# Recording the first and second group norms in three steps instead of two, with the scale pinned on VectorE

## Chip, core and metric

The kernel runs on one core of a Trainium2 chip. Time is device microseconds of one launch, the median of several runs; the profile is one execution, with the span from its first to its last instruction. The core has five engines with a queue each: TensorE (PE: matmuls, with weight loads shown as PEld), VectorE (DVE), ScalarE (ACT), GpSimd (POOL) and SyncE (SP), which here only issues DMAs.

## What is computed

Two bottleneck blocks on an input of 64 images, 1024 channels, 14 x 14 positions. The first has batch norms over the whole batch; the second is deformable and has group norms, one set of statistics for each image and group:

```python
# first block
out = relu(_bn(_conv(x, w1, b1, 1, 0), g1, be1))
out = relu(_bn(_conv(out, w2, b2, 1, 1), g2, be2))
out = softplus(residual_scale)[0] * _bn(_conv(out, w3, b3, 1, 0), g3, be3)
x = relu(x + out)
# second block
out = relu(group_norm(conv(x, w1), gn1_scale, gn1_bias))
om = conv(out, w_off, pad=1) + b_off
sampled = bilinear_sample(out, py(om), px(om)) * sigmoid(om[:, 18:])
out = einsum('bckhw,ock->bohw', sampled, w2)
out = relu(group_norm(out, gn2_scale, gn2_bias))
out = group_norm(conv(out, w3), gn3_scale, gn3_bias)
return relu(out + x)
```

with

```python
def group_norm(x, scale, bias, groups=32, eps=1e-05):
    xg = x.reshape(B, groups, C // groups, H, W)
    m = xg.mean(axis=(2, 3, 4), keepdims=True)
    v = xg.var(axis=(2, 3, 4), keepdims=True)
    xn = ((xg - m) * rsqrt(v + eps)).reshape(B, C, H, W)
    return xn * scale + bias
```

## The kernel before

**Stages.** The first block takes roughly the first 970 us. The change is in the second, which goes through the batch in 32 pairs of images (`NP` = 32, `p` is the number of a pair; a tile row holds 2 x 196 positions). It is a software pipeline written out by hand: `slot(t)` does the sampling and the second convolution of pair t, and beside them the first convolution, the first norm and the offset convolution of pair t+1, and the second norm, the third convolution and the third norm of pair t-1. `fill()` stands ahead of the first slot, `tail()` behind the last. In slots 0 and 1 there is no first convolution (`d1` is empty), since `fill()` has done it.

**Order.** Each stage is a list of small functions ("steps"). `put(steps, extra, at)` places each of `extra` ahead of the step whose number is in `at`, and `weave` mixes two lists evenly; the calls of all of them in turn are the recorded order. Inside the slots only TensorE follows that order as recorded (`manual_schedule` names PE alone); for VectorE, ScalarE, GpSimd and SyncE a scheduler orders the instructions by its own estimate of when their inputs are there, earlier recorded ones first. `tc.keep_in_program_order(ins)` ties one instruction: it stays behind the instruction that was recorded last on its engine. In `tail()` PE, VectorE, GpSimd and ScalarE all follow the recorded order.

**The norm.** `Norm` keeps the statistics of one pair. `stats` (L1004) are `bn_stats` on VectorE, one for each image and block of 128 channels. `total` (L1015) is a transpose. `mean` is five VectorE instructions (L1025 to L1036). `root` is one on VectorE (L1041, maximum and epsilon) and a power on GpSimd (L1042). `scale` is a transpose (L1048) and three small instructions (L1057, L1060, L1063) on VectorE, which leave factor `sc` and shift `sh` for the activations on ScalarE. `scale` has a parameter `tie` for the transpose. `finish` is `root` and `scale`, one right behind the other. The third norm has its own steps (`total`, `mean`, `root`, `end`), with the scale tied; the first and second have `mean` and `finish`.

**What lies around it in a slot from t = 2 to t = 30**, in recorded order. First `d1`, 16 steps of two matmuls each (L1099): block 0 (steps 0 to 7), then block 1 (8 to 15); at the end of a block ScalarE copies the result (L1107) and VectorE takes its statistics. Into this list go the second norm's steps, at 6 the late output of pair t-2 (two sums on VectorE, L1745, each with an activation on ScalarE, L1747, and then the store, L1773, issued by SyncE), and at 10 the products for the first set of taps (`corners`, L1392, tied). The four activations of the second norm are L1576; from them GpSimd makes the sums T (L1592 to L1596).

Then come the sampling matmuls (`sp`, L1412, copied out by ScalarE, L1420) woven with the first half of the third convolution (`d`, L1655), 24 steps, and into them goes the first norm of pair t+1. The third convolution has seven products for each j, m = 0 to 6, in three banks of PSUM. Products 0 and 1 give E (copied by ScalarE, L1659). Products 2 and 3 give V on VectorE (L1662: bank plus E). After product 4 GpSimd makes two sums from V (L1667: a new E, and part of z). After product 5 VectorE writes z (L1671). Product 6 adds into the bank that V is read from, and L1675 writes the rest of z. In this list the products of j = 0 are steps 0, 2, 4, 6, 7, 9 and 11, those of j = 1 begin at step 12. The first norm's activations (L1122) go to steps 14, 16, 18 and 21; they feed the transforms (L1163, L1167) for the offset convolution (`om`, L1187).

The tiles z are two buffers, one for each half of the channels, which change owner every slot: the new z can be written when the old one's output has been stored.

Of the kernel before, what the change touches and what calls it, by code (L numbers as in the profile page):

```python
# [22 lines left out]
MB = 2  # L23
# [21 lines left out]
def kernel(  # L45
# [197 lines left out]
    with ExitStack() as l, tc.manual_schedule(  # L243
# [127 lines left out]
        for n in range(K):  # L371
            q, j = divmod(n, HB)
# [88 lines left out]
    with upool, tc.manual_schedule(  # L461
# [11 lines left out]
        sp = pool(upool, "s", 4)  # L473
# [181 lines left out]
    with l0, tc.manual_schedule(  # L655
# [107 lines left out]
        for p in range(2, NP - 2, 2):  # L763
            tt = Ts
            for j in range(HB):
                acc = [ps.tile([P, N2], FP, tag=f"ps{m}", name=f"c3_{p}_{j}_{m}") for m in range(4)]
                part = ts(j, P)
# [157 lines left out]
    def build_second_bottleneck(l1, path, run, early):  # L925
# [56 lines left out]
        class Norm:  # L982
# [79 lines left out]
                )  # L1062
                nc.vector.tensor_tensor(self.sh, self.sh, beta, ALU.add)  # L1063

            def finish(self):
                self.root()
                self.scale()

        pairs = {}
# [10 lines left out]
        def residual(p, b0=0, b1=CB):  # L1082

            for b in range(b0, b1):

                tc.keep_in_program_order(end_of_first(p, Z0, b))
                relu_of_first(p, b)

        def first_conv(p, by_inputs=False):
# [22 lines left out]
                order.sort(key=lambda v: v[1])  # L1112
            return [lambda o=o, c=c: step(o, c) for o, c in order]

        def first_norm(p):
            q = pairs[p]

            def relu(c, i):
                n, a1 = q["gn1"], q["a1"]

                tc.keep_in_program_order(
                    nc.scalar.activation(  # L1122
                        a1[:, c, ts(i, HW)],
                        a1[:, c, ts(i, HW)],
                        AF.Relu,
                        bias=n.sh[:, c, i : i + 1],
                        scale=n.sc[:, c, i : i + 1],
                    )
                )
                if i == 1:  # L1130
                    transform(p, c)

            return [lambda: q["gn1"].mean(), lambda: q["gn1"].finish()] + [
                lambda c=c, i=i: relu(c, i) for c in range(MB) for i in range(2)
            ]

# [432 lines left out]
        def second_norm(p, m=0):  # L1569

            q = pairs[p]

            def relu(c, i):
                n, h2 = q["gn2"][m], q["h2"]
                b = c - n.b0
                nc.scalar.activation(  # L1576
                    h2[:, c, ts(i, HW)],
                    h2[:, c, ts(i, HW)],
                    AF.Relu,
                    bias=n.sh[:, b, i : i + 1],  # L1580
                    scale=n.sc[:, b, i : i + 1],
                )

            def sums():
                if p == NP - 1:
                    return
                h2 = q["h2"]
                T3 = q["T3"] = {
                    m: one.tile([P, HW], FP, tag=f"T{m}", name=f"T{m}_{p}") for m in (1, 2, 4)
                }  # L1590
                (b11, b12), (b21, b22) = ([h2[:, c, ts(i, HW)] for i in range(2)] for c in range(2))
                nc.gpsimd.tensor_tensor(T3[1], b12, b11, ALU.subtract)  # L1592
                nc.gpsimd.tensor_tensor(T3[2], b22, T3[1], ALU.subtract)

                nc.gpsimd.tensor_tensor(b12, b22, b12, ALU.subtract)
                nc.gpsimd.tensor_tensor(T3[4], b21, T3[2], ALU.subtract)  # L1596

            order = ((0, 0), (0, 1), (1, 1), (1, 0))
            if p == NP - 1:
                order = ((m, 0), (m, 1))  # L1600
            return (
                [lambda: q["gn2"][m].mean(), lambda: q["gn2"][m].finish()]
                + [lambda c=c, i=i: relu(c, i) for c, i in order]
                + [sums]
            )
# [175 lines left out]
        def weave(a, b):  # L1781

            both = [((n + 0.5) / len(l), m, s) for m, l in enumerate((a, b)) for n, s in enumerate(l)]
            return [s for _, _, s in sorted(both, key=lambda v: v[:2])]

        def put(steps, extra, at):

            done, at = [], at[: len(extra)]
            for n, s in enumerate(steps):
                done += [extra[m] for m, k in enumerate(at) if k == n]  # L1790
                done.append(s)
            return done + [extra[m] for m, k in enumerate(at) if k >= len(steps)]
# [11 lines left out]
        def slot(t):  # L1804
# [5 lines left out]
            def part(yes, stage, *args):  # L1810
                return stage(*args) if yes else []
# [7 lines left out]
            for e in range(2, E):  # L1819
                sp[e - 2].append(lambda e=e: this and (list(spread_rows(t, e)), list(spread_columns(t, e)), corners(t, e)))  # L1820
            d1 = part(front and not (early and t < 2), first_conv, t + 1)
            norm1, norm2, norm3 = (
                part(front, first_norm, t + 1)[2 if early and t == 1 else 0 :],
                part(back, second_norm, t - 1),
                part(back, third_norm, t - 1),
            )
# [9 lines left out]
            om = part(front, offset_conv, t + 1) + part(front, selection, t + 1) + loads  # L1836
            half = len(d3) // 2
            if d1:
                extra = list(zip((5, 8, 12, 12, 13, 13, 14), norm2)) + [(10, w) for w in weights[:1]]
                extra = sorted(extra + [(6, s) for s in late], key=lambda v: v[0])  # L1840
                todo = put(d1, [s for _, s in extra], [k for k, _ in extra])
                todo += put(weave(sp[0], d3[:half]), norm1, (4, 7, 14, 16, 18, 21))
                todo += weights[1:] + d3[half : half + 2] + om
                todo += weave(sp[1], d3[half + 2 :])
            else:
                extra = list(zip((3, 6, 8, 9, 10, 10, 10), norm2)) + list(zip((0, 0, 1, 1), norm1))
                extra = sorted(
                    extra + [(9, w) for w in weights[1:]] + [(4, s) for s in late], key=lambda v: v[0]
                )
                todo = put(sp[0], [s for _, s in extra], [k for k, _ in extra])  # L1850
                todo += om + weave(sp[1], d3[:half]) + d3[half:]
# [28 lines left out]
            extra = []  # L1880
            if early and t == 0:

                extra += list(zip((5, 11), first_norm(2)))
            if bare:
                extra.append((n - 6, lambda: corners(t + 1, 0)))
            if back and t < NP - 1:
# [2 lines left out]
                extra.append((3, lambda: output(t - 1, 1)))  # L1889
            if t == NP - 1:  # L1890

                extra += list(zip([n // 2 + k for k in (3, 5, 6, 6)], ends2))
            extra.sort(key=lambda v: v[0])
            todo += put(pd[E - 1], [s for _, s in extra], [k for k, _ in extra])
            if ahead:
# [4 lines left out]
        def tail():  # L1900

            p = NP - 1
            mean, finish2, *relus = second_norm(p, 1)[:-1]
            d3 = plain_third_conv(p)

            def products(first, end):
                for step in d3[first:end]:
                    step()

            def ends(n, b0, b1):  # L1910
                for b in range(b0, b1):
                    finish(p, n, b)

            products(0, 3)
            mean()
            products(3, 5)
            finish2()
            for step in relus:
                step()
            products(5, 10)  # L1920
            n0, n1, n2 = pairs[p]["gn3"]
            n0.total()
            products(10, 12)
            n0.mean()
            products(12, 14)
            n0.root()
            n1.total()
            products(14, 15)
            n1.mean()
            n0.scale()  # L1930
            products(15, 16)
            n1.root()
            n2.total()
            n2.mean()
            ends(n0, 0, 1)
            n2.root()
            n1.scale()
            ends(n0, 1, 4)
            store(p, 0, 4)
            n2.scale()  # L1940
            ends(n1, 0, 2)
            store(p, 4, 6)
            ends(n2, 0, 2)
            store(p, 6, 8)
# [11 lines left out]
        def fill():  # L1956

            for p in range(3):
                start(p)
            load_h3(2, Z0)  # L1960
            steps = first_conv(0, by_inputs=True)
            norm = first_norm(0)
            steps += put(
                first_conv(1),
                norm[:2] + [offset_weights] + norm[2:] + offset_conv(0) + selection(0),
                (3, 5, 5, 6, 6, 6, 6) + (12,) * (MB * 3) + (12,),
            )
            norm, (distances, end) = first_norm(1), factors(0)
            steps += [lambda: pairs[1]["gn1"].total(), lambda: residual(2, 0, 3)] + transposes(0)

            steps += norm[:1] + [lambda: residual(2, 3, 7), distances, lambda: residual(2, 7), end]

            def spread():

                for e in range(2):
                    for n, _ in enumerate(zip(spread_rows(0, e), spread_columns(0, e))):
                        if e == n == 0:
                            lend(0)

            steps += [spread]  # L1980
            steps += put(
                first_conv(2),
                norm[1:]
                + [lambda: sums_of_second(0, 3), lambda: corners(0, 0)]
                + offset_conv(1)
                + selection(1)
                + [lambda: sums_of_second(6)],
                (3, 7, 7, 8, 8, 11, 11) + (12,) * (MB * 3) + (14, 16),
            )
            for step in steps:  # L1990
                step()
# [94 lines left out]
```

## Time and profile before

| | |
|---|---|
| median of 3 runs | 2870.07 us (2866.82 to 2872.13) |
| profiled execution | 2869.56 us, its span 2867.8 us |
| mean granted TensorE clock | 0.992 |
| busy, share of the span: PE / PEld | 97% / 70% |
| VectorE / ScalarE / GpSimd | 82% / 46% / 32% |
| DMA, mean rate over the span | 148 GB/s |

A timeline row gives start, length, engine, line and operation, then what is written from what, with partitions and elements, and how many instructions the row merges; in brackets stands the idle time of the engine ahead of it and what ended that. Instructions of one engine can overlap by a little, and TensorE's ends are modelled, so durations on TensorE are best taken from start to start.

### The profile page before, as it was taken

The numbers are of one execution on the slowest core, as the hardware profiler recorded it, in microseconds if no ns is written. First come the engines' busy times: TensorE is split into PE (matmuls) and PEld (weight loads), VectorE is DVE, ScalarE is ACT, GpSimd is POOL, SyncE is SP. The second block draws the span as 40 slices with busy tenths as digits, with TensorE's granted clock in tenths as the row PEclk, the third lists the DMA queues.
The fourth block names the chain that finished last, engine by engine and source line by source line (L and its number), as shares of the span: only waits on it lengthen the run. The fifth ranks groups of instructions, "written<-read, shape, count | busy, mean of one in ns | idle before, by whom it ended". The sixth has DMA issues, their size and how long they took to land.

```text
span 2867.8 us, 39785 instructions
## 1 busy us (share of the span) xinstructions
PE 2769.3 (97%) x12930; PEld 2008.4 (70%) x12930; DVE 2353.6 (82%) x5284; ACT 1324.2 (46%) x2723; POOL 918.1 (32%) x1069
## 2 busy tenths in 40 slices
PE   9999899998999999999999999999999999999996
PEld 5555555555555578877887788778877788778864
DVE  7877899997888778878888888878888888888876
ACT  0000221213555545655565556555555556555654
POOL 4631466664666212222212221222222222222221
PEclk9999999999999999999999999999999999999998
DMA  7665000004555444554555455544555455545541
GB/s 232 187 179 169 15 1 1 1 1 175 217 197 193 152 159 164 172 175 136 186 165 185 142 162 177 188 151 151 182 182 163 140 191 172 175 137 190 166 135 53
DMA packets 350286, 424.21 MB, mean 148 GB/s; under 512 B 27860, under 2 KB 292468, under 8 KB 349812
## 3 DMA queue, kind: packets, MB, share of 16 engines
q1 hardware_dynamic: 350068, 421.57, 44.9%
q8 instruction: 104, 1.70, 0.3%
q14 instruction: 114, 0.93, 0.1%
HBM read 296.49 MB, written 116.76 MB: 144 GB/s over the span
## 4 chain that ended last, share of the span: by engine, by line
PE 24%; DVE 15%; ACT 13%; issue 5%; DMA 5%; POOL 3%; SPq 1%; DVEq 0%; POOLq 0%; ACTq 0%
PE sp L1412 9%; PE d L1655 8%; ACT z L1723 7%; PE pd L1524 5%; ACT h L228 4%; DVE st L1004 2%; PE om L1187 2%; DMA X<-wd 2%; DVE S L1392 2%; DMA out_dram<-z 2%; DVE z L1745 1%; DVE wt L1253 1%; ACT wt L1254 1%; ACT wt L1255 1%; DVE V L1662 1%
## 5 line engine op out<-in xcount | busy, mean ns | idle before, releaser
L1412 PE MATMUL sp<-S,aT 126*128 126x420 f32 (+3 forms) x1536 | 486.7, 415 | 9.3 <-DVE S L1392 6.6
L1420 ACT COPY sm<-sp 128x336 f32<-128x336 f32 (+3 forms) x640 | 285.8, 451 | 264.6 <-PE sp L1412 239.6
L1524 PE MATMUL pd<-sm,w2b_sb 128*128 128x196 f32 x2232 | 400.6, 329 | 0.0
L1524 PEld LDWEIGHTS pd<-sm,w2b_sb 128*128 128x128 f32 x2232 | 371.3, 190 | 0.0
L534 PE MATMUL c<-v,u_sb 128*128 128x392 f32 x1024 | 343.1, 497 | 10.6 <-DVE bn1sh L167 8.2
L1099 PE MATMUL d<-h,w1b_sb 128*128 128x392 f32 x1024 | 343.9, 493 | 3.7 <-ACT h L228 3.7
L1524 PE MATMUL pd<-sm,Sc 128*128 128x196 f32 x1674 | 308.1, 329 | 0.0
L534 PEld LDWEIGHTS c<-v,u_sb 128*128 128x128 f32 x1024 | 194.6, 191 | 159.1 <-DVE v L520 11.7
L1099 PEld LDWEIGHTS d<-h,w1b_sb 128*128 128x128 f32 x1024 | 193.1, 190 | 139.9 <-ACT h L228 7.9
L1480 DVE TENSOR_TENSOR sm<-sm 128x980 f32<-128x980 f32 (+2 forms) x257 | 268.4, 1055 | 19.4 <-PE pd L1524 8.1
L1524 PEld LDWEIGHTS pd<-sm,Sc 128*128 128x128 f32 x1674 | 278.7, 190 | 0.2
L1412 PEld LDWEIGHTS sp<-S,aT 126*128 126x128 f32 x1536 | 256.5, 191 | 22.9 <-ACT sm L1420 7.1
L1723 ACT ACTIVATE z<-z,gn_0sh,gn_0sc 128x196 f32<-128x196 f32 x496 | 222.5, 537 | 44.7 <-DVE gn_0sh L1063 44.7
L520 DVE TENSOR_TENSOR v<-t 128x392 f32<-128x392 f32 x256 | 193.0, 812 | 0.0
L1555 POOL TENSOR_TENSOR E<-V,E 128x196 f32<-128x196 f32 x31 | 18.7, 605 | 542.5 <-DVE V L1554 542.5
L1655 PE MATMUL d<-h,w3b_sb 128*128 128x196 f32 x744 | 176.4, 332 | 1.0 <-ACT h L1576 1.0
L1667 POOL TENSOR_TENSOR E<-V,E 128x196 f32<-128x196 f32 x124 | 74.3, 600 | 306.9 <-DVE V L1662 304.0
L1655 PEld LDWEIGHTS d<-h,w3b_sb 128*128 128x128 f32 x744 | 131.4, 189 | 56.6 <-issue 18.9
L1747 ACT ACTIVATE z<-z 128x784 f32<-128x784 f32 x124 | 102.6, 853 | 127.4 <-DVE z L1745 127.2
L1392 DVE TENSOR_TENSOR S<-S,X 126x840 f32<-126x840 f32 (+1 forms) x192 | 148.7, 824 | 10.1 <-DMA X<-wd 9.4
L389 PE MATMUL c<-xc,w1a_sb 128*128 128x392 f32 x384 | 149.1, 497 | 5.4 <-DMA xc<-in_x_dram 5.4
L1004 DVE BATCH_NORM_STATS2 st<-z 128x6 f32<-128x196 f32 x496 | 151.6, 352 | 3.2
(684 smaller groups left out, 4936.4 us busy)
## 6 DMA issues: line engine op xcount, KB each, us to landing
xc<-in_x_dram SPq DMA_DIRECT2D x128, 392.0 KB
h<-o SPq DMA_DIRECT2D x64, 784.0 KB
h<-in_x_dram SPq DMA_DIRECT2D x64, 784.0 KB
h<-h SPq DMA_DIRECT2D x64, 784.0 KB
out_dram<-z SPq DMA_DIRECT2D x126, 392.0 KB
X<-wd SPq DMA_DIRECT2D x64, 413.4 KB
S<-wd SPq DMA_DIRECT2D x64, 413.4 KB
S<-wd SPq DMA_DIRECT2D x64, 330.8 KB
```

Of the source, the lines that this page charges most:

```text
L389: nc.tensor.matmul(acc[m], a, b, start=(j == 0), stop=(j == HB - 1))
L520: nc.vector.tensor_tensor(v[:, u].rearrange("p (i y x) -> p i y x", y=7, x=7), cols[c][:, :, i : i + 13 : 2, :], cols[c][:, :, j : j + 13 ...
L534: nc.tensor.matmul(m[u], u_sb[:, c, u, k % 4, ts(o, P)], vts[k][c][:, u], start=(c == 0), stop=(c == MB - 1),)
L1004: last = nc.vector.bn_stats(rows[:, :, 2 * b + i], src[:, ts(i, HW)])
L1099: nc.tensor.matmul(q["pt"][o], w1b_sb[:, c, ts(o, P)], q["y"][:, c, :], start=(c == 0), stop=(c == CB - 1),)
L1392: nc.vector.tensor_tensor(S[:, piece], S[:, piece], X(piece), ALU.mult)
L1412: nc.tensor.matmul(pt[:, i], q["aT"][:, i0 + i, c, starts.index(r0), :], q["S"][e][g, r0][:, :, i0 + i, :], start=(j == 0), stop=(j == len ...
L1420: nc.scalar.copy(dst, pt.rearrange("p i k n -> p k i n"))
L1480: return nc.vector.tensor_tensor(dst, a, b, ALU.subtract)
L1524: nc.tensor.matmul(bank[:, m % 2], a[:, k], b[:, k - k0],  start=(k == 0 and m in (5, 0, 2, 6)), stop=(k == T - 1), skip_group_check=True,)
L1655: nc.tensor.matmul(bank[:, m % 2 if m < 6 else 1], a, b, start=(m < 6), stop=True, skip_group_check=True)
L1723: nc.scalar.activation(z[:, ts(i, HW)], z[:, ts(i, HW)], AF.Identity, bias=n.sh[:, b, i : i + 1], scale=n.sc[:, b, i : i + 1],)
```

## The change

The methods of `Norm` stay, `finish` goes. A new function `norm_steps` gives three steps in place of two: mean; root; scale with its transpose tied behind what was recorded last on VectorE. All places that list the first and second norm's steps are changed to that: the root goes where the mean is, the scale where the pair of root and scale was, or one step behind it (8 instead of 7 for the first norm in the slots). In the fill, the root of pair 1 moves ahead of the residual sums and of the distances. In the tail the root moves ahead of two products.

```diff
-            def finish(self):
-                self.root()
-                self.scale()
-
...
+        def norm_steps(norm):
+
+            return [
+                lambda: norm().mean(),
+                lambda: norm().root(),
+                lambda: norm().scale(tc.keep_in_program_order),
+            ]
+
         def first_norm(p):
...
-            return [lambda: q["gn1"].mean(), lambda: q["gn1"].finish()] + [
+            return norm_steps(lambda: q["gn1"]) + [
                 lambda c=c, i=i: relu(c, i) for c in range(MB) for i in range(2)
             ]
...
             return (
-                [lambda: q["gn2"][m].mean(), lambda: q["gn2"][m].finish()]
+                norm_steps(lambda: q["gn2"][m])
                 + [lambda c=c, i=i: relu(c, i) for c, i in order]
                 + [sums]
             )
...
-                part(front, first_norm, t + 1)[2 if early and t == 1 else 0 :],
+                part(front, first_norm, t + 1)[3 if early and t == 1 else 0 :],
...
             if d1:
-                extra = list(zip((5, 8, 12, 12, 13, 13, 14), norm2)) + [(10, w) for w in weights[:1]]
+                extra = list(zip((5, 5, 8, 12, 12, 13, 13, 14), norm2)) + [(10, w) for w in weights[:1]]
                 extra = sorted(extra + [(6, s) for s in late], key=lambda v: v[0])
                 todo = put(d1, [s for _, s in extra], [k for k, _ in extra])
-                todo += put(weave(sp[0], d3[:half]), norm1, (4, 7, 14, 16, 18, 21))
+                todo += put(weave(sp[0], d3[:half]), norm1, (4, 4, 8, 14, 16, 18, 21))
...
             else:
-                extra = list(zip((3, 6, 8, 9, 10, 10, 10), norm2)) + list(zip((0, 0, 1, 1), norm1))
+                extra = list(zip((3, 3, 6, 8, 9, 10, 10, 10), norm2)) + list(zip((0, 0, 1, 1), norm1))
...
-                extra += list(zip((5, 11), first_norm(2)))
+                extra += list(zip((5, 5, 11), first_norm(2)))
...
-                extra += list(zip([n // 2 + k for k in (3, 5, 6, 6)], ends2))
+                extra += list(zip([n // 2 + k for k in (3, 3, 5, 6, 6)], ends2))
...
-            mean, finish2, *relus = second_norm(p, 1)[:-1]
+            mean, root, scale, *relus = second_norm(p, 1)[:-1]
...
             products(0, 3)
             mean()
+            root()
             products(3, 5)
-            finish2()
+            scale()
...
             steps += put(
                 first_conv(1),
-                norm[:2] + [offset_weights] + norm[2:] + offset_conv(0) + selection(0),
-                (3, 5, 5, 6, 6, 6, 6) + (12,) * (MB * 3) + (12,),
+                norm[:3] + [offset_weights] + norm[3:] + offset_conv(0) + selection(0),
+                (3, 3, 5, 5, 6, 6, 6, 6) + (12,) * (MB * 3) + (12,),
             )
...
-            steps += norm[:1] + [lambda: residual(2, 3, 7), distances, lambda: residual(2, 7), end]
+            steps += norm[:2] + [lambda: residual(2, 3, 7), distances, lambda: residual(2, 7), end]
...
                 first_conv(2),
-                norm[1:]
+                norm[2:]
```

## The prediction

> **What bounds the kernel now.** I read the page, the PE waits, the timeline of one slot, and then single waits in other slots. TensorE is busy 2769.3 of 2867.8 us. From 1098.6 us on, 29 slots of the pipeline follow each other with first convolutions in them (from the first matmul of L1099 in one to that in the next), nearly all 57.91 us long. I write "at 17.1" for 17.1 us after that first matmul, which lies at 1387.85 in the slot shown. The stretch table gives that slot, in us with PE busy first; behind it stands the view of the PE waits from 1150 to 2720 (us in total, times, longest):
>
> ```profile
> 1387.85:1445.76 57.91, 56.65 (x320) 46.17 (x320) 47.40 (x118) 33.37 (x72) 13.24 (x19) 1.00 0.52 162
> ```
> ```profile
> PE d L1655 <- DVE V L1662: 32.9, 27, 1.2
> PE d L1655 <- DVE z L1671: 0.9, 2, 0.5
> PE d L1655 <- ACT h L1576: 0.2, 1, 0.2
> ```
>
> So TensorE sets the pace, and one wait per slot is nearly all its idle time: 1.22 us before product 6 of the third convolution's first block. The timeline (start, length, idle time and releaser in brackets) shows why:
>
> ```profile
> 1403.11 1.01 POOL L1042 TENSOR_TENSOR gn_8G<-gn_8G,mhalf 128x4 f32<-128x4 f32 x1 [1.14 <-DVE gn_8G L1041]
> 1403.75 0.64 PE L1412 MATMUL sp<-S,aT 126*128 126x140 f32 x4
> 1404.15 0.25 DVE L1048 STREAM_TRANSPOSE gn_8B<-gn_8G 128x64 f32<-128x64 f32 x1 [1.12 <-POOL gn_8G L1042]
> 1404.90 0.56 DVE L1662 TENSOR_TENSOR V<-d,E 128x392 f32<-128x392 f32 x1
> 1405.61 0.57 PE L1655 MATMUL d<-T,w3b_sb 128*128 128x196 f32 x2 [1.22 <-DVE V L1662]
> 1406.35 0.64 PE L1412 MATMUL sp<-S,aT 126*128 126x140 f32 x4
> 1406.83 0.50 PE L1655 MATMUL d<-T,Sb 128*128 128x196 f32 x2
> ```
>
> The root of the first norm goes to GpSimd (L1042), VectorE stands still 1.12 us until it is back, does the four instructions of the scale, and only then V. Product 6 writes into the bank that V reads. V was recorded before the scale and runs behind it: outside TensorE the recorded order is not the order of the engines.
>
> **First norm, part by part.** No instruction is added or removed. Mean and root stay at position 4, the scale goes to 8 and is pinned behind V. V needs product 3 (in the row of four at 1402.05) and the copy of E (done 1401.36), so it can run when the root ends on VectorE, 1403.03, and is done by 1403.6. The root comes back at 1404.12 as now, so the scale ends at 1404.98 as now; its first reader starts at 1407.32, far behind. TensorE's price from start to start: from the four sp matmuls to the next d pair takes 1405.61 - 1403.75 = 1.86 us here and 1406.83 - 1406.35 = 0.48 unhindered, so **1.38 us a slot** go. Bounds: 0 (V is late for another reason; a loss would need V behind 1404.90, and nothing of the norm stands ahead of it any more) to 1.38; I take 1.38, since V's inputs are there 0.5 us ahead.
>
> **Second norm.** Its rows now:
>
> ```profile
> 1395.21 0.17 DVE L1041 TENSOR_SCALAR gn_6G<-gn_6G 128x4 f32<-128x4 f32 x1
> 1395.27 0.47 ACT L1107 COPY a<-d 128x392 f32<-128x392 f32 x1
> 1395.45 1.02 POOL L1042 TENSOR_TENSOR gn_6G<-gn_6G,mhalf 128x4 f32<-128x4 f32 x1 [4.93 <-DVE gn_6G L1041]
> 1395.63 0.86 ACT L1747 ACTIVATE z<-z 128x784 f32<-128x784 f32 x1
> 1396.51 0.24 DVE L1048 STREAM_TRANSPOSE gn_6B<-gn_6G 128x64 f32<-128x64 f32 x1 [1.13 <-POOL gn_6G L1042]
> 1396.52 1.87 SPq L1773 DMA_DIRECT2D out_dram<-z  x2
> 1396.67 0.59 DVE L1004 BATCH_NORM_STATS2 st<-a 128x6 f32<-128x196 f32 x2
> ```
>
> The root moves ahead of the two late output sums (L1745, 0.97 us each, 1393.44 to 1395.21), so GpSimd works beside them. But at position 8 the last vector work recorded is not the sum: step 7 of the first convolution records the statistics of its block 0 (L1004), so the scale is pinned behind those. They wait for ScalarE's copy (1395.27 + 0.47, some 0.2 later now since the root's 0.17 + 0.03 stands ahead of the sums): statistics 1396.0 to 1396.6, scale 1396.65 to 1397.45 against 1397.72 now. So 0.27 us of the 1.13 is won, not all. Behind the scale queue the products S (L1392) and, on ScalarE, the four activations of h (1397.75), then T on GpSimd. TensorE waits for T: product 0 to 1 takes 1.17 us and 1 to 2 1.35, against 1.04 unhindered in block 1 (1406.83 to 1407.87), 0.44 together. Bounds of this part: -0.6 (copy behind the second activation L1747, 0.86 later) to +0.44; I take **+0.3**.
>
> **What is late next.** TensorE now reaches block 1 1.68 us sooner, and there stands the late store. The second half of z is stored at 8.67 and 9.10 (the L1773 row), and L1671, which writes the next z, must wait for it. In another slot:
>
> ```profile
> 1698.16 0.57 DVE L1671 TENSOR_TENSOR z<-d,E 128x392 f32<-128x392 f32 x1 [2.49 <-DMA out_dram<-z]
> 1698.79 0.60 PE L1655 MATMUL d<-T,Sb 128*128 128x196 f32 x2 [0.55 <-DVE z L1671]
> ```
>
> TensorE follows 0.63 us behind L1671's start; unhindered that product starts at 20.02 (1407.87), so L1671 does no harm up to 19.39 now, and up to 19.39 - 1.68 = 17.71 afterwards. The last of the store's 16 semaphore updates comes, in the 28 slots from 1155.99 on, at 16.3, 16.8, 16.8, 17.2, 17.6, 17.8, 17.9, 18.0, 18.0, 18.1, 18.2, 18.2, 18.2, 18.5, 18.6, 18.6, 18.6, 18.7, 18.7, 18.7, 18.8, 18.8, 18.8, 18.8, 19.2, 19.4, 19.8 and 20.0; L1671 follows 0.13 later. Now 4 slots lose 1.4 us to it in all. Afterwards each landing adds (landing + 0.13 - 17.71) where that is positive: 23.9 us in 24 slots. This assumes that stores stay where they are counted from the slot's start; what feeds the queue ahead of them is issued behind the place where time is saved, in the slot before. The store itself gets later by the root (0.2) and by what the next row shows of a root beside two-input vector work:
>
> ```profile
> 1370.42 2.46 DVE L1480 TENSOR_TENSOR sm<-sm 128x980 f32<-128x980 f32 x2
> 1370.46 1.56 POOL L1042 TENSOR_TENSOR gn_0G<-gn_0G,mhalf 128x1 f32<-128x1 f32 x1 [5.02 <-DVE gn_0G L1041]
> ```
>
> A root of this size takes 0.56 us elsewhere (2816.49); here it ends 0.42 us behind the first sum's end, and the second sum starts some 0.1 us late. So 0.3 us for the store in the slots where SyncE is not late anyway: stalls of 25.8 us. [...]
>
> **Sum**, against the profiled execution (2869.56 us, span 2867.8; the median of 2870.07 is 0.5 higher): 28 x 1.68 = 47.0, plus 1.4 of stalls that are in the old time, minus 25.8, is 22.7; the slot at 1098.60 adds 0.8. In the fill, wt x mk (L1260, 1004.30) stands behind the scale of gn1_1, which waits 1.12; now it is ahead, and TensorE waits at 1013.97 for what it feeds: 0 to 1.05, I take 0.8. The rest is nothing: in the tail and in the last slot's own norm no vector work is recorded between root and scale (L1048 keeps its 1.12 and 1.19); in the slot from 2780 the scale of gn_30 ends 0.9 sooner, but ScalarE is busy until 2794.2 with older work (if not, 0.8 gained). 22.7 + 0.8 + 0.8 = 24.3, hence **2845 us**, 2836 to 2856 by these bounds.
>
> **Rivals.**
> Full gain: stores land a microsecond sooner relative to TensorE and only the V wait counts: 29 x 1.68 + 1.4 + 0.8 = 51, 2819. For it: landings scatter by 3.7 us for reasons in the queue. Against: stores can't be issued sooner than the sums allow.
> Consumed: the store gets 1.5 us later (both activations L1747 behind other ScalarE work); the same formula leaves 0.06 us a slot, 2867. Here the V wait is gone from the profile and L1671's is in its place.
> The root holds up the second late sum for its whole 1.02 us: store 1.2 to 1.3 later, some 9 us left, 2860.
> Slower: the pinned statistics slip between the two late sums on VectorE. Then the second sum waits for ScalarE's copy (to 1395.95), two statistics (0.6) and its own 0.97: it ends some 2 us later, so do activation and store; the formula gives -0.39 us a slot, 29 x 0.39 = 11, 2881. It decides from 1.5 us of delay on. For it: VectorE's order is not the recorded one, and statistics already sit inside the scale (1396.67). Against: both sums are pinned behind the root and are ready long before the copy.
>
> **Chances.** Forecast 0.50, full gain 0.12, root in the way 0.08, consumed 0.11, slower 0.19. A difference under 0.2% (5.7 us) can't be told from none here. Faster 0.50 + 0.12 + 0.08 = 0.70; within 0.2% 0.11; slower 0.19. The range takes in all but the slower case: 2817 to 2871.
>
> **What would show it.** Right: no wait of d L1655 for V in the slots; V directly behind L1041, L1048 of gn1 idle about 0.5 us instead of 1.12; L1671's wait for out_dram<-z in some 24 slots instead of 10 (14.3 us in all now, by the view of VectorE's waits), with waits of PE for L1671 of 0.2 to 2.4 us; slots of about 57.1 us that scatter. Wrong: PE still waits for V (V late for another reason), L1773 issued over 1 us later than 8.67 (the sums' order), or uniform slots of 56.2 (the store is no limit).

## The result and the profile after

| | before | after |
|---|---|---|
| median of 6 runs each | 2869.89 us (2866.82 to 2872.13) | 2847.79 us (2837.11 to 2854.74) |
| ratio after to before, 95% interval | | 0.9923, 0.9901 to 0.9945 |
| span of the profiled execution | 2867.8 us | 2845.4 us |

The change saves 22 us (0.8%). The times after scatter over 18 us where those before scatter over 5.

The page of the changed kernel begins:

```profile
span 2845.4 us, 39785 instructions
...
PE 2764.5 (97%) x12930; PEld 2013.2 (71%) x12930; DVE 2372.7 (83%) x5284; ACT 1328.2 (47%) x2723; POOL 936.5 (33%) x1069
```

TensorE is still the engine that sets the pace. Its waits from 1150 to 2700 us (total in us, times, longest) are now one single line, with another releaser. (All lines of the sampling and the convolutions have moved by 4: L1655, L1662, L1671 are now L1659, L1666, L1675; the third norm's output sums, activations and store are L1749, L1751 and L1777.)

```profile
PE d L1659 <- DVE z L1675: 20.6, 22, 2.8
```

VectorE's own waits in the same stretch name what is behind it (before, out_dram<-z stood there with 14.3 us, 10 times):

```profile
DVE z L1675 <- DMA out_dram<-z: 31.0, 22, 3.3
...
DVE st L1004 <- ACT a L1103: 12.8, 27, 0.5
```

So the wait for V is gone from all slots, and the wait of z for the old tile's store has taken its place in most of them. The stretch table (length, then busy time of PE, PEld, DVE, ACT and POOL with counts, granted clock, DMA share, GB/s) shows two slots, one with that wait and one without:

```profile
1383.08:1439.71 56.63, 56.37 (x320) 46.25 (x319) 48.04 (x118) 33.50 (x72) 13.86 (x19) 1.00 0.53 169
...
2073.40:2129.50 56.10, 56.10 (x319) 46.31 (x319) 48.05 (x118) 33.42 (x72) 13.86 (x19) 1.00 0.53 169
```

In the second TensorE has no idle time at all. I call 56.10 the floor; before, it was 57.91 with 1.22 us of idle time in it. The 28 slots from the one at 1099.59 on (1098.60 before, up to the first matmul at 2699.68 and 2721.60) last 56.10 to 60.82 us, 1600.1 in all against 1623.0 before. That is 22.9 us less: 28 x 1.81 = 50.7 from the floor, 1.5 that stood above the floor before, minus 29.3 that stands above it now.

**First norm**, by the timeline of the slot at 1383.08 (start, length, idle time and releaser in brackets):

```profile
1397.75 0.17 DVE L1041 TENSOR_SCALAR gn_8G<-gn_8G 128x4 f32<-128x4 f32 x1
1397.83 0.57 DVE L1666 TENSOR_TENSOR V<-d,E 128x392 f32<-128x392 f32 x1
1397.99 1.01 POOL L1042 TENSOR_TENSOR gn_8G<-gn_8G,mhalf 128x4 f32<-128x4 f32 x1 [1.14 <-DVE gn_8G L1041]
...
1398.64 0.64 PE L1416 MATMUL sp<-S,aT 126*128 126x140 f32 x4
...
1399.04 0.25 DVE L1048 STREAM_TRANSPOSE gn_8B<-gn_8G 128x64 f32<-128x64 f32 x1 [0.64 <-POOL gn_8G L1042]
1399.12 0.50 PE L1659 MATMUL d<-T,w3b_sb 128*128 128x196 f32 x2
```

V runs directly behind L1041, while GpSimd makes the root; VectorE is idle 0.64 us instead of 1.12. From the four sp matmuls to the next pair of d it takes 1399.12 - 1398.64 = 0.48 us, exactly the unhindered distance, and 1.86 before.

**Second norm**, same slot:

```profile
1388.84 0.17 DVE L1041 TENSOR_SCALAR gn_6G<-gn_6G 128x4 f32<-128x4 f32 x1
1388.91 1.85 DVE L1749 TENSOR_TENSOR z<-z,h 128x784 f32<-128x784 f32 x2
1389.09 1.67 POOL L1042 TENSOR_TENSOR gn_6G<-gn_6G,mhalf 128x4 f32<-128x4 f32 x1 [3.29 <-DVE gn_6G L1041]
...
1390.74 0.47 ACT L1103 COPY a<-d 128x392 f32<-128x392 f32 x1
...
1391.24 0.63 DVE L1004 BATCH_NORM_STATS2 st<-a 128x6 f32<-128x196 f32 x2 [0.47 <-ACT a L1103]
1391.78 0.23 DVE L1048 STREAM_TRANSPOSE gn_6B<-gn_6G 128x64 f32<-128x64 f32 x1
1391.99 1.25 SPq L1777 DMA_DIRECT2D out_dram<-z  x2
...
1392.64 1.88 ACT L1580 ACTIVATE h<-h,gn_6sh,gn_6sc 128x196 f32<-128x196 f32 x4 [0.67 <-DVE gn_6sh L1063]
```

The root lies beside the two late sums, then VectorE waits 0.47 us for ScalarE's copy, takes the statistics of block 0, and only then comes the scale: the order that the pin demands. The activations of h begin at 1392.64 - 1383.08 = 9.56 us of the slot, 9.90 before. The second store is issued at 8.91, 8.67 before.

**The store**, same slot: L1675 waits 0.76 us for it, and TensorE waits behind L1675.

```profile
1401.10 0.57 DVE L1675 TENSOR_TENSOR z<-d,E 128x392 f32<-128x392 f32 x1 [0.76 <-DMA out_dram<-z]
...
1401.72 0.60 PE L1659 MATMUL d<-T,Sb 128*128 128x196 f32 x2 [0.26 <-DVE z L1675]
```

The last update of the store comes at 16.6 to 20.3 us of the slots, 18.3 on average, as before (16.3 to 20.0, 18.3). A slot with the landing at 17.29 us is 56.11 long, one at 17.75 56.48, one at 18.58 57.31, one at 19.53 58.26: from 17.4 on every microsecond of landing is a microsecond of slot (the longest slot lost more, see the last section).

### The profile page after: what moved, and what is told of

Read it like the earlier page. It is cut to its first block, busy times and chain, and to the rows that moved or that the text cites. A ratio compares the mean times of both kernels' runs of the same rounds, so it can differ in the third digit from the quotient of the medians.

```text
span 2845.4 us, 39785 instructions
## 1 busy us (share of the span) xinstructions
PE 2764.5 (97%) x12930; PEld 2013.2 (71%) x12930; DVE 2372.7 (83%) x5284; ACT 1328.2 (47%) x2723; POOL 936.5 (33%) x1069
## 4 chain that ended last, share of the span: by engine, by line
PE 36%; DMA 12%; DVE 8%; ACT 4%; issue 2%; SPq 2%; POOL 1%; DVEq 0%; ACTq 0%; POOLq 0%
PE pd L1528 15%; PE sp L1416 8%; PE d L1659 7%; DMA out_dram<-z 7%; DMA S<-wd 2%; PE d L1095 2%; DMA aT<-aT 2%; PE om L1191 2%; DVE st L1004 2%; ACT z L1727 1%; SPq L1379 1%; ACT h L228 1%; DVE z L1675 1%; PE tr L1294 1%; DMA X<-wd 1%
## 5 line engine op out<-in xcount | busy, mean ns | idle before, releaser
L1659 PE MATMUL d<-h,w3b_sb 128*128 128x196 f32 x744 | 174.6, 330 | 0.8 <-ACT h L1580 0.8
L1659 PEld LDWEIGHTS d<-h,w3b_sb 128*128 128x128 f32 x744 | 133.8, 189 | 51.8 <-issue 19.1
L1751 ACT ACTIVATE z<-z 128x784 f32<-128x784 f32 x124 | 103.2, 860 | 133.1 <-DVE z L1749 133.0
L1671 POOL TENSOR_TENSOR E<-V,E 128x196 f32<-128x196 f32 x124 | 74.4, 600 | 265.0 <-DVE V L1666 260.2
L1004 DVE BATCH_NORM_STATS2 st<-z 128x6 f32<-128x196 f32 x496 | 151.6, 352 | 3.2
```

The lines of the kernel that those rows point to most:

```text
L1004: last = nc.vector.bn_stats(rows[:, :, 2 * b + i], src[:, ts(i, HW)])
L1659: nc.tensor.matmul(bank[:, m % 2 if m < 6 else 1], a, b, start=(m < 6), stop=True, skip_group_check=True)
```

## The experiments

The kernel before was timed again beside the experiments: 2871.5 us beside the four recorded first (first norm alone, second norm alone, no pin, no late store), 2870.1 beside the other three. All times are medians; ratios are to the kernel before, with 95% intervals. Waits are those from 1150 to 2660 us; in that stretch the changed kernel has 20.2 us of waits for z, and the kernel before 31.7 for V.

### First norm alone, second norm alone

In the first kernel the second norm keeps root and scale together and untied, as before:

```diff
-                norm_steps(lambda: q["gn2"][m])
+                [
+                    lambda: q["gn2"][m].mean(),
+                    lambda: None,
+                    lambda: (q["gn2"][m].root(), q["gn2"][m].scale()),
+                ]
...
             mean()
-            root()
             products(3, 5)
```

> The first norm in three pinned steps, the second norm recorded as before (mean, then root and scale together, not pinned). Theory (the pin behind V frees 1.38 us of TensorE a slot, the second norm adds 0.4, and the late store takes part back): the shortest slots are 57.91 - 1.38 = 56.5 us, no wait of PE for V, waits of PE for L1671's successor on out_dram<-z in some 20 slots of 0.1 to 2 us, total 2846 to 2852. Rival (the second norm's earlier scale is what pulls V forward): slots stay at 57.9, PE goes on waiting about 1.2 us for V, total 2868 to 2872.

In the second it is the first norm that keeps them together, at position 7:

```diff
-            return norm_steps(lambda: q["gn1"]) + [
+            return [
+                lambda: q["gn1"].mean(),
+                lambda: None,
+                lambda: (q["gn1"].root(), q["gn1"].scale()),
+            ] + [
...
-                todo += put(weave(sp[0], d3[:half]), norm1, (4, 4, 8, 14, 16, 18, 21))
+                todo += put(weave(sp[0], d3[:half]), norm1, (4, 4, 7, 14, 16, 18, 21))
```

> The second norm in three pinned steps, the first norm recorded as before. Theory: VectorE's chain is 0.35 us earlier, PE still waits over 1 us for V in each slot, shortest slots 57.5 us, the store stalls stay near 3 us in all, total 2860 to 2864. Rival (the second norm does it): slots of 56.1 to 57, wait for V under 0.3 us, total 2845 to 2852.

Measured: first norm alone 2852.95 us, 0.993 (0.9918 to 0.9942); second norm alone 2864.22 us, 0.9974 (0.9964 to 0.9983). TensorE's waits, first norm alone (there the line numbers lie 4 higher still):

```profile
PE d L1663 <- DVE z L1679: 22.2, 17, 3.5
```

and second norm alone:

```profile
PE d L1663 <- DVE V L1670: 31.7, 26, 1.2
PE d L1663 <- DVE z L1679: 3.2, 5, 1.3
```

Of the two parts it is the first norm's that takes the wait for V away; with the second's alone it stays. The floors tell the sizes: 56.44 us with the first norm alone, so it is worth 57.91 - 56.44 = 1.47 us a slot; 57.50 with the second alone, 0.41. Together they make 1.88, where the full change has 1.81. The totals of both expectations held but for 1 us of the first (2853 against at most 2852). Its profiled execution, the slowest of the six, has a stall of 3.52 us in one slot, of which more below.

### The split without the pin

```diff
-                lambda: norm().scale(tc.keep_in_program_order),
+                lambda: norm().scale(),
```

> The changed kernel with the scale not tied (same three steps, same places in the list). Theory: V stands behind the scale of the first norm again, so the stall on the root is back in front of V; but the second norm's scale, no longer tied behind the statistics, comes up to 1 us sooner and takes VectorE's chain with it, so PE waits 0.3 to 1.2 us for V. Total 2850 to 2866. Rival (recording the root early is enough, the pin does nothing): no wait for V, total as the changed kernel, 2840 to 2852.

Measured: 2852.96 us, 0.994 (0.9928 to 0.9952). TensorE's waits:

```profile
PE d L1659 <- DVE V L1666: 19.4, 26, 1.1
PE d L1659 <- DVE z L1675: 8.9, 10, 1.6
```

VectorE in one slot:

```profile
1398.05 0.17 DVE L1041 TENSOR_SCALAR gn_8G<-gn_8G 128x4 f32<-128x4 f32 x1
1399.33 0.24 DVE L1048 STREAM_TRANSPOSE gn_8B<-gn_8G 128x64 f32<-128x64 f32 x1 [1.12 <-POOL gn_8G L1042]
...
1400.08 0.57 DVE L1666 TENSOR_TENSOR V<-d,E 128x392 f32<-128x392 f32 x1
```

Without the pin VectorE's order puts the scale ahead of V again, although it is recorded behind V, and the 1.12 us of standing still are back. The floor is 56.92 against 56.10, so the two pins are worth 0.82 us a slot. Without them the wait for V still shrinks from 1.22 to 0.75 us a slot (19.4 / 26): the slot shown starts at 1384.02, so L1041 comes at 14.03 us of it instead of 15.01, while TensorE's row of four products comes at 13.85 instead of 14.20. Of the 23 us of floor that the pins bring (0.82 x 28) the changed kernel keeps only about 5 (2852.96 against 2847.79, ratios whose intervals overlap): its 28 slots stand 29.3 us above their floor, those without the pins 12.5, and its waits for z are 20.2 us in place of 8.9.

### The late store left out

```diff
-            store(p, half * HB, half * HB + HB)
+            if half == 0 or p >= NP - 2:
+                store(p, half * HB, half * HB + HB)
```

> The changed kernel without the store of the second half of the channels for all pairs but the last two; that part of the output is left out. Theory (what is left of the gain is taken by L1675 waiting for that store): every slot is 56.1 us, no wait for out_dram<-z in the slots, total 29 us below the changed kernel, 2816 to 2822, and runs agree within 2 us. Rival (VectorE's own queue or GpSimd makes L1675 late, the store only comes last by chance): PE goes on waiting for L1675 in over half the slots, total 2835 to 2850.

Measured: 2814.32 us, 0.9802 (0.979 to 0.9815). No wait of TensorE is left in the slots from 1150 us on, and all but two of the 28 (56.37 and 56.44) are within 0.05 us of each other:

```profile
1384.00:1440.05 56.05, 56.05 (x320) 46.31 (x319) 47.94 (x119) 33.38 (x71) 13.85 (x19) 1.00 0.46 150
```

The changed kernel had 29.3 us above its floor, and 2847.79 - 2814.32 = 33.5 us go with the store (1.4 of them in the fill, which no store of this kind touches). So it is the store, and not the sums or activations ahead of it (which are all still there), that eats more than half of the gain. The transfers of that store are gone too, though; the move of the late output below keeps them, and the waits go all the same.

### The second norm untied

The first norm keeps its pin; the second is split, but not tied:

```diff
-        def norm_steps(norm):
+        def norm_steps(norm, tie=tc.keep_in_program_order):
...
-                lambda: norm().scale(tc.keep_in_program_order),
+                lambda: norm().scale(tie),
...
-                norm_steps(lambda: q["gn2"][m])
+                norm_steps(lambda: q["gn2"][m], lambda v: v)
```

> The changed kernel with the second norm's scale not tied; the first norm's is. Theory (the second norm's pin puts the scale behind the statistics of the first convolution, which wait for ScalarE's copy): the scale ends 0.5 to 0.9 us sooner, the four activations of h start at 8.7 to 9.1 instead of 9.56, the shortest slots lose at most the 0.05 us that T still costs, and the store stalls eat that: total 2840 to 2852, not to be told from the changed kernel. Rival (the pin matters for the second norm too): total 4 us or more above the changed kernel.

Measured: 2849.44 us, 0.9935 (0.9921 to 0.9949), not to be told from the change. The scale now runs ahead of the statistics:

```profile
1387.51 0.24 DVE L1048 STREAM_TRANSPOSE gn_6B<-gn_6G 128x64 f32<-128x64 f32 x1
1388.07 0.62 DVE L1004 BATCH_NORM_STATS2 st<-a 128x6 f32<-128x196 f32 x2
...
1388.79 1.88 ACT L1580 ACTIVATE h<-h,gn_6sh,gn_6sc 128x196 f32<-128x196 f32 x4
```

This slot starts at 1379.85, so the activations of h begin at 8.94 instead of 9.56. The floor falls from 56.10 to 55.91, where at most 0.05 was expected, and the medians show nothing of it. (The profiled execution of this kernel is 6.2 us shorter than that of the change, spans of 2839.2 and 2845.4, but it was the fastest of five whose times scatter over 14 us.) So the pin of the first norm is worth 56.92 - 55.91 = 1.01 us of floor, and that of the second costs 0.19; that the store hides these 0.19 is likely, since the slots stand 30.6 us above the floor here and 29.3 in the change, but the medians are too close together to show it.

### The late output moved forward

If the store is the limit, it should be issued sooner. Here the output of the second half of z no longer waits for the next slot's first convolution, but follows the first half's in its own slot:

```diff
-            late = [lambda: output(t - 2, 1)] if t >= 2 else []
+            late = [lambda: output(t - 2, 1)] if t == NP - 1 else []
...
+                if t < NP - 2:
+                    extra.append((n * 20 // 28, lambda: output(t - 1, 1)))
```

> The changed kernel with the output of the second half of the channels recorded in the slot before, behind that of the first half, so that its sums fill VectorE's idle 1.9 us ahead of the second convolution's V. Theory: the store is issued 3 to 5 us sooner (4 to 6 us into the slot instead of 8.9), lands before 17.5, L1675 stops waiting for it in most slots; shortest slots 56.0, total 2814 to 2828. Rival (the landing is set by the transfers ahead in the queue, not by the issue): it lands as late as now, slots scatter from 56.1 to 58, total 2842 to 2850.

Measured: 2812.61 us (2811.26 to 2813.3), 0.9799 (0.9786 to 0.9812), 1.4 us below the expected range and faster than both kernels. Slot and waits of TensorE:

```profile
1377.37:1433.28 55.91, 55.91 (x320) 46.40 (x319) 48.18 (x119) 33.56 (x72) 13.20 (x19) 1.00 0.53 172
```
```profile
PE d L1659 <- DVE z L1675: 1.4, 4, 0.6
```

The store is two DMAs, one for each image; on average the first is issued at 6.6 us of the slot and the second at 8.1, against 9.2 and 9.7 in the change, so later than the 4 to 6 us of the expectation. The last update of the store now comes at 16.4 us of the slot on average instead of 18.3, and 24 of the 28 slots are at the floor of 55.91. So the landing does follow the issue, and the rival is refuted. The scatter of the times has shrunk to 2 us.

### The same move in the kernel before

The same two edits, without the change:

> The kernel before with that one move of the late output and nothing else. Theory (the store cost the kernel before only 1.4 us; what the move brings there is VectorE time ahead of the second norm): PE still waits for V, 0.5 to 0.9 us a slot, since the root stands in front of it; slots near 56.9, total 2836 to 2850, some 24 above the changed kernel with the same move. Rival (the store was the limit all along and the pin adds nothing once it is gone): no wait for V, total within 5 us of the changed kernel with the move.

Measured: 2826.13 us, 0.9845 (0.9832 to 0.9859): 10 us faster than the lowest that was expected. TensorE's waits:

```profile
PE d L1655 <- DVE V L1662: 8.4, 27, 0.4
PE d L1655 <- DVE z L1671: 0.6, 2, 0.3
```

The miss lies in the wait for V: 0.31 us a slot where 0.5 to 0.9 was expected. The two sums (1.85 us) no longer stand ahead of the norms on VectorE, so in one slot L1041 of the first norm comes 13.55 us behind the first matmul (15.01 before), while TensorE reaches the row of four products at 13.65 (14.20 before). VectorE won 1.46 us, TensorE 0.55; 1.22 - 0.91 = 0.31 is what remains of the wait. So the move alone brings 44 us to the kernel before, twice what the change brings. Little of that is the store, which cost that kernel about 1.5 us; 28 x (57.91 - 56.45) = 41 us are the floor, that is VectorE's earlier norms. On top of it the change is worth 2826.13 - 2812.61 = 13.5 us. That fits the floors, 56.45 and 55.91: 28 x 0.54 = 15. The wait as it is listed understates what it costs: from the four sp matmuls to the next pair of d it is 1398.39 - 1397.45 = 0.94 us in this kernel against 0.48 unhindered, 0.46 of the 0.54.

## Why the prediction was right

The forecast was 2845 us (2836 to 2856), 24.3 us less than the profiled execution before. Measured are 2847.79 us, and a span that is 22.4 us shorter.

**First norm.** Right: V stands behind L1041, the wait is gone from all slots, and 1.38 us is to the hundredth what one slot shows between the two PE rows. By the floor of the kernel with this part alone it is 1.47. One detail of the text was wrong: the first norm's root doesn't stay at position 4, it moves there from 7. In the kernel before, L1041 already stood right behind the mean's last instruction (1402.61 + 0.22 = 1402.83, start 1402.86), so nothing in the sum hung on it.

**Second norm.** Right in order and sign: the statistics of block 0 wait for ScalarE's copy and hold up the scale. It was mis-sized by a little: 0.35 us sooner at the scale's end against 0.27, and 0.43 us of the floor (1.81 - 1.38) against the 0.3 taken, just inside the bound of 0.44. With this part alone it is 0.41.

**The root beside the late sums.** It took 1.67 us instead of 1.02, and the two sums still took 1.85 together: the root was held up, the sums were not. So the store came 0.24 us later (0.3 taken), and the rival in which the root blocks the second sum is refuted.

**The store.** The mechanism was right, and taking the store away showed it: 28 slots scatter from 56.1 to 60.8 us, 24 of them above the floor. The term was mis-sized: 29.3 us instead of 25.8. Two sizes moved. The harmless landing lies at 17.4 us and not at 17.58, most of it since TensorE gets there 1.81 us sooner and not 1.68; by the measured landings this makes about 27 us. The other 2 us are one slot with a slower clock (0.65 behind its stall, below). The 1.9 us that were added for a later store (25.8 against 23.9) don't show: where SyncE is free it is issued 0.24 us later, but the mean of the landings is 18.3 in both traces. The floor was also better than predicted, 50.7 instead of 47.0, so that 50.7 + 1.5 - 29.3 = 22.9 stands against 47.0 + 1.4 - 25.8, which is 22.6 and not the 22.7 of the sum. The two misses cancel, and they belong together: whatever TensorE gains ahead of a landing that stays, it waits away there. The prediction put the scatter of the landings down to the queue; the trace shows that much of it is when SyncE issues the store. The last update comes 7.2 to 9.1 us behind the issue of the second DMA; in the 13 slots in which the first is issued by 9.0 us it comes at 17.7 us on average, in the 15 others at 18.9. In the longest slot the store is issued at 10.98, behind two transfers of X that SyncE issues ahead of it (1.95 us from 1850.72 on), although the last activation ends at 1850.72.

**The fill.** This step failed. 0.8 us was taken as a gain; the fill (first matmul of the first convolution at 968 us to the first slot) is 131.6 us long against 129.9. TensorE's rows in the kernel before:

```profile
1013.97 4.04 PE L1412 MATMUL sp<-S,aT 126*128 126x420 f32 x16 [1.63 <-DVE S L1392]
...
1020.11 1.30 PE L1412 MATMUL sp<-S,aT 126*128 126x420 f32 x3 [2.10 <-DVE S L1392]
```

and in the changed kernel, with the vector instruction that it waits for:

```profile
1012.89 4.04 PE L1416 MATMUL sp<-S,aT 126*128 126x420 f32 x16 [0.62 <-DVE S L1396]
1018.76 1.03 DVE L1396 TENSOR_TENSOR S<-S,X 126x840 f32<-126x840 f32 x1 [2.88 <-DMA X<-wd]
1019.94 0.94 PE L1416 MATMUL sp<-S,aT 126*128 126x420 f32 x2 [3.01 <-DVE S L1396]
```

The first wait did fall by 1.0 us, as predicted. But the next one is for a transfer of X, which came no sooner, and took the microsecond back: what is late next was asked for the slots, not for the fill. TensorE's idle time in the fill is 9.2 us in both kernels (129.88 - 120.70 and 131.62 - 122.42). The 1.7 us by which the fill is longer are busy time, and the granted clock accounts for them: behind the wait of 2.10 us in the kernel before it stays at 1.00, behind that of 3.01 us it is 0.64 over 4.50 us, which loses 0.36 x 4.50 = 1.6 us. The stretches of 4.5 us behind the two waits, before and after:

```profile
1020.11:1024.61 4.50, 4.26 (x12) 2.28 (x13) 4.12 (x11) 2.36 (x5) 0.00 (x0) 1.00 0.59 223
```
```profile
1019.94:1024.44 4.50, 4.18 (x7) 2.05 (x8) 4.23 (x11) 2.03 (x6) 0.00 (x0) 0.64 0.54 202
```

That this loss belongs to the change is not shown: the kernel before with the output moved, whose fill is untouched, has a wait of 3.22 us at the first of the two places, a clock of 0.65 behind it and a fill of 131.5 us, and the eight other fills lie between 129.9 and 131.7.

**Small terms.** The slot at 1098.60, which is one of the 28 above, won 1.0 us (0.8 predicted). The prediction counted its 28 from 1155.99 on; from there to the first sp matmul behind the last slot (2782.26 and 2759.38) the gain is 22.9 us too. What comes behind that matmul is 0.5 us longer, and the stretch ahead of the fill 0.7 us shorter, which nothing here explains. 22.9 + 1.0 + 0.7 - 1.7 - 0.5 = 22.4, the difference of the spans. So what the 22.4 us lack to the 24.3 forecast is the fill's miss of 2.5 us, less three gains of 0.2 each. That the median came within 3 us of the forecast is in part luck, for the six times scatter over 18.

**The rivals.** Full gain (2819) is what one gets only with the store out of the way: 2814 without it, 2813 with it sooner. Consumed fell with a store only 0.24 us later, not 1.5. The slower case needed the statistics between the two sums; both sums run behind each other in 1.85 us, ahead of the statistics.

## What to carry to other kernels

Recording an instruction later does not by itself move it on an engine whose order a scheduler sets (without the pin the scale still ran at 1399.33, ahead of V at 1400.08): look where it stands in the trace, and pin it behind the work that is to hide it, not behind work that waits for yet another engine. Before an engine's wait is taken away, list the landing times of every transfer that the engine meets next: a landing that stays turns each microsecond won ahead of it into a wait (here 29.3 us stood above the floor where 50.7 had been won). When the old idle time reappears as a wait for a DMA, move the work that issues that DMA; here that took another 35 us off the changed kernel (2847.79 to 2812.61).

## What the runs showed of the hardware that was not expected

**Three stalls of 2.12 to 3.52 us cost almost 2 us more each.** The longest slot of the changed kernel, 60.82 us, has one stall of 2.76 us:

```profile
1862.36 0.57 DVE L1675 TENSOR_TENSOR z<-d,E 128x392 f32<-128x392 f32 x1 [3.26 <-DMA out_dram<-z]
1862.98 0.60 PE L1659 MATMUL d<-T,Sb 128*128 128x196 f32 x2 [2.76 <-DVE z L1675]
```

60.82 - 56.10 - 2.76 = 1.96 us are missing. The stretch of 4.5 us behind that stall has a granted clock (the first number behind the counts) of 0.65:

```profile
1862.98:1867.48 4.50, 4.50 (x13) 3.45 (x14) 3.01 (x10) 2.88 (x7) 1.64 (x3) 0.65 0.00 0
```

In the kernel with the first norm alone a stall of 3.52 us at 1405.12 and one of 1.99 at 1812.70 stand side by side:

```profile
1405.12:1409.62 4.50, 4.50 (x13) 3.45 (x14) 3.01 (x10) 2.76 (x7) 1.64 (x3) 0.64 0.00 0
...
1812.70:1817.20 4.50, 4.50 (x20) 3.42 (x20) 3.72 (x12) 3.73 (x8) 1.64 (x3) 1.00 0.00 0
```

The first of these slots is 61.92 us long: 56.44 + 3.52 + 1.96. The kernel with the second norm untied has a stall of 2.12 us with a clock of 0.62 behind it, in a slot of 59.98: 55.91 + 2.12 + 1.95. So in these slots the clock stayed at 1.00 behind the stall of 1.99 us and fell behind those of 2.12, 2.76 and 3.52, at a price of 1.95 or 1.96 us each. In the fill the length of the wait alone does not decide: 2.10 us in the kernel before left 1.00, 1.88 in the changed kernel with the output moved left 0.65.

The traces of the two kernels show what went with it. In the changed kernel half clock begins at 1021.23 and at 1864.32 us and lasts 3.41 us both times, with 1.00 ahead of it and behind; it begins again at 2758.61. These starts are 247 and 262 times 3.413 us apart, so I read the traces in steps of that length. Around the longest slot's stall three steps read:

```profile
1860.91:1864.32 3.41, 1.34 (x6) 1.01 (x7) 1.93 (x6) 1.30 (x3) 0.00 (x0) 1.00 0.01 4
1864.32:1867.73 3.41, 3.41 (x9) 2.58 (x8) 1.81 (x7) 1.82 (x5) 1.64 (x3) 0.50 0.00 0
1867.73:1871.15 3.42, 3.42 (x56) 2.49 (x54) 3.42 (x9) 1.10 (x3) 0.29 (x1) 1.00 0.02 5
```

TensorE is idle for 2.07 us of the first step, and the next one runs at half clock. From 970 to 2750 us the traces before and after have one other step with over 1.67 us of idle time, 2.44 us in the fill of the changed kernel (1017.82 to 1021.23), and half clock follows that too; behind the steps with 1.67 us or less the clock is 1.00. The 2.10 us in the fill of the kernel before fell on two steps, 0.68 and 1.42 us, and cost no clock.

**The second norm's root took 0.65 us longer beside the sums than beside statistics.** L1042 took 1.67 us beside the two sums L1749, and 1.02 us in the kernel with the output moved, where it lies beside L1004. Two small vector instructions took longer beside GpSimd in turn: L1057 and L1060 of the first norm's scale took 0.27 and 0.52 us in the changed kernel while GpSimd made its sums from V (L1671 there, 1398.97 to 1400.13), and 0.16 each in the second norm's scale, where GpSimd stood idle.
